# Turning tiles with 32x32 transposes on VectorE and copies inside SBUF, instead of transposes on TensorE

## Chip, core, metric

One core of a Trainium2 chip. The metric is the device time of one execution in microseconds (us). Every kernel here ran several times. Ratios to the kernel before are the mean time of the one kernel's fast runs over that of the other's fast runs of the same rounds, so they are not quite the ratios of the medians that are quoted.

## The reference, cut to what matters

64 graphs of 256 nodes with 256 features pass through four layers of graph networks. Each starts with the same norm and adds its result to `x`:

```python
h = jnp.maximum(_layernorm(x, axis=-1), 0.0)
x = x + layer(h, adj, ...)
# layer 0: 8-head attention with a mask;  layer 1: one-head graph attention
# layer 2: three steps of message passing and a GRU cell, on the state h
#   m = h @ weight[i];  aggr = A^T m;  h = gru(aggr, h)
# layer 3: 4-head graph attention
```

All is float32. The kernel takes two graphs at a time, a "pair": 32 pairs of 4 tiles of 128 tokens each (T = 4, D = 256, P = 128, N2 = 512).

## The kernel before

The kernel's code hands its matmuls operands whose summed dimension lies on the partitions, and the products with weights sum over the features. So every normalised tile is turned, from tokens on the partitions to features on the partitions. In layer 2 the state is kept with features on the partitions, and is turned back into tokens after each step. Both turns are TensorE transposes into PSUM, evicted by VectorE or ScalarE.

```python
        for g in range(2):                      # in norm_relu_T; tokens=True in layer 2 only
            def scaled(g=g):                    # (x - mean) * rstd: ScalarE if tokens, else VectorE
                ...
        hT = w4()
        for k in range(2):
            ps = bank()
            def turn(k=k, ps=ps):
                for t in range(T):
                    nc.tensor.transpose(ps()[:, t * P : (t + 1) * P], tok(xn())[:, t, k * P : (k + 1) * P], ident)
            add((PE, 4 * TURN, turn), reads=[xn], writes=[ps], claims=[hT])
            ...                                 # evicted, with the ReLU, to hT[:, k, :]
# in layer2, after each of the three steps:
            for g in range(2):
                ps = bank()
                def tokens(g=g, ps=ps, hT=hT):  # 4 transposes of the state
                    ...
                add((PE, 4 * TURN, tokens), reads=[hT], writes=[ps], claims=[h] if h else [])
                ...                             # evicted to h, or added to x after the last step
```

The order of all instructions is made while the program is built. Each task is given to `add` with an engine, the time that it is taken to occupy that engine, and a latency until its result can be read. The ordering then takes, again and again, the task that can begin first, over several pairs at once, and emits the tasks in that order.

```python
    def add(self, forms, reads=(), writes=(), latency=0.0, claims=()):
        ...
            free[engine] = begin + us                                   # in order()
            t.begin, t.end, t.engine = begin, begin + us + t.latency, engine
...
    SLOTS = {   # tag: (tiles, shape, type, tiles kept back for the oldest pair)
        "adj": (2, [P, T * N], I32, 1),
        "w4": (20, [P, T * D], FP, 6),
        "w8": (4, [P, 8, N], FP, 1),
        "mask": (4, [P, T * N], BF, 1),
        "ps": (8, [P, 512], FP, 2),
        ...
```

## Time and profile before

| | before |
|---|---|
| time, median of 3 | 4326.73 us (4326.27 to 4327.57) |
| TensorE busy, granted clock | 98%, 0.996 |
| VectorE, ScalarE, GpSimd busy | 68%, 53%, 14% |
| f32 transposes removed by the change | 1,792 |

In the lines shown, L414 is line 414 of that kernel's file, `w` stands for its 4 KB tiles, and SPq is SyncE's queue. An issue is the instruction that starts one copy. Its landing is counted from the start of the issue until the data are there. The granted clock is the share of full speed that TensorE's clock had.

The prediction below shows the lines. In TensorE's rows the end of one matmul overlaps the start of the next (in the run before, a 512-wide matmul of L761 has 0.59 us, and the next starts 0.43 us after it), so the measure used throughout is the distance between the starts of successive matmuls.

### The profile page before, as it was taken

The numbers are of one execution on the slowest core, as the hardware profiler recorded it, in microseconds if no ns is written. First come the engines' busy times: TensorE is split into PE (matmuls) and PEld (weight loads), VectorE is DVE, ScalarE is ACT, GpSimd is POOL, SyncE is SP. The second block draws the span as 40 slices with busy tenths as digits, with TensorE's granted clock in tenths as the row PEclk, the third lists the DMA queues.
The fourth block names the chain that finished last, engine by engine and source line by source line (L and its number), as shares of the span: only waits on it lengthen the run. The fifth ranks groups of instructions, "written<-read, shape, count | busy, mean of one in ns | idle before, by whom it ended". The sixth has DMA issues, their size and how long they took to land.

```text
span 4324.5 us, 56216 instructions
## 1 busy us (share of the span) xinstructions
PE 4244.1 (98%) x20720; PEld 2631.3 (61%) x20720; DVE 2930.0 (68%) x5426; ACT 2301.1 (53%) x6105; POOL 590.3 (14%) x582
## 2 busy tenths in 40 slices
PE   7999999999999999999999999999999999999997
PEld 5665566656656665666566566656655665666564
DVE  6775577667657755876676577558765765776554
ACT  4664465545545644655455456446554554564444
POOL 1111111111111111111111111111111111111111
PEclk9999999999999999999999999999999999999999
DMA  2000011000000000010000000000100100000000
GB/s 83 21 18 22 20 36 34 20 16 24 30 25 25 13 28 25 30 35 20 11 30 30 25 25 13 27 25 26 40 11 17 32 30 25 25 13 28 15 15 15
DMA packets 109986, 108.47 MB, mean 25 GB/s; under 512 B 7312, under 2 KB 109712, under 8 KB 109712
## 3 DMA queue, kind: packets, MB, share of 16 engines
q1 hardware_dynamic: 109712, 104.89, 7.6%
q8 instruction: 163, 2.67, 0.3%
q14 instruction: 111, 0.91, 0.1%
HBM read 88.09 MB, written 16.78 MB: 24 GB/s over the span
## 4 chain that ended last, share of the span: by engine, by line
PE 77%; DVE 8%; issue 8%; ACT 5%; POOL 1%; SPq 0%; DMA 0%; POOLq 0%; ACTq 0%; DVEq 0%
PE ps L761 36%; PE ps L775 7%; PE ps L518 5%; PE ps L480 5%; PE ps L573 4%; PE ps L717 3%; PE ps L654 3%; PE ps L540 2%; PE ps L457 2%; PE ps L614 2%; PE ps L840 2%; PE ps L858 2%; ACT w L886 2%; ACT w L494 2%; DVE w L823 1%
## 5 line engine op out<-in xcount | busy, mean ns | idle before, releaser
L761 PE MATMUL ps<-w,whhT 128*128 128x512 f32 x2304 | 1080.3, 595 | 0.7 <-DVE w L402 0.4
L761 PE MATMUL ps<-w,giT 128*128 128x512 f32 x2304 | 1063.6, 593 | 0.0
L494 ACT ACTIVATE w<-w,mx 128x256 f32<-128x256 f32 x1664 | 825.7, 503 | 186.3 <-DVE mx L561 128.9
L401 ACT COPY w<-ps 128x512 f32<-128x512 f32 x983 | 553.0, 587 | 657.3 <-PE ps L775 290.8
L761 PEld LDWEIGHTS ps<-w,giT 128*128 128x128 f32 x2304 | 433.6, 190 | 523.9 <-issue 513.3
L761 PEld LDWEIGHTS ps<-w,whhT 128*128 128x128 f32 x2304 | 415.3, 190 | 406.6 <-issue 383.9
L811 POOL TENSOR_TENSOR w<-w,w 128x512 f32<-128x512 f32 x192 | 251.2, 1317 | 1689.6 <-ACT w L806 1331.8
L402 DVE COPY w<-ps 128x512 f32<-128x512 f32 x553 | 366.4, 684 | 153.7 <-PE ps L573 58.0
L786 ACT ACTIVATE w<-ps,brz 128x512 f32<-128x512 f32 x192 | 131.8, 687 | 463.2 <-PE ps L761 460.3
L791 DVE TENSOR_SCALAR w<-w 128x512 f32<-128x512 f32 x192 | 81.6, 425 | 407.8 <-ACT w L786 407.7
L554 DVE SCALAR_TENSOR_TENSOR w<-ps,mask 128x512 f32<-128x512 f32 x512 | 333.3, 680 | 33.9 <-PE ps L540 33.9
L775 PE MATMUL ps<-w,w 128*128 128x256 f32 x1536 | 355.7, 379 | 0.0
L775 PEld LDWEIGHTS ps<-w,w 128*128 128x128 f32 x1536 | 286.2, 190 | 60.7 <-issue 22.9
L494 ACT ACTIVATION_READ_ACCUMULATOR w<-w,mx 128x1 f32 x1664 | 322.9, 194 | 0.0
L823 DVE SCALAR_TENSOR_TENSOR w<-w,w 128x512 f32<-128x512 f32 x192 | 152.5, 794 | 246.3 <-ACT w L818 240.7
L561 DVE TENSOR_REDUCE mx<-w 128x4 f32<-128x1024 f32 x256 | 309.2, 1208 | 2.0
L573 PE MATMUL ps<-ident,w 128*128 128x128 f32 x2048 | 269.4, 273 | 0.6
L573 PEld LDWEIGHTS ps<-ident,w 128*128 128x128 f32 x2048 | 235.1, 140 | 57.1 <-issue 25.6
L818 ACT ACTIVATE w<-ps,brz 128x512 f32<-128x512 f32 x192 | 130.8, 681 | 235.0 <-PE ps L761 234.9
L424 POOL TENSOR_SCALAR rs<-mv 128x4 f32<-128x4 f32 x128 | 33.6, 262 | 1354.8 <-DVE mv L417 1293.5
L886 ACT ACTIVATE w<-w,f 128x256 f32<-128x256 f32 x512 | 217.1, 503 | 1.4
L445 DVE TENSOR_SCALAR w<-x,mv,rs 128x256 f32<-128x256 f32 x384 | 185.3, 541 | 16.5 <-POOL rs L425 15.8
(113 smaller groups left out, 5633.0 us busy)
## 6 DMA issues: line engine op xcount, KB each, us to landing
adj<-in_adj_dram SPq DMA_DIRECT2D x128, 512.0 KB, 4.1
x<-in_x_dram SPq DMA_DIRECT2D x64, 256.0 KB, 2.8
out_dram<-x SPq DMA_DIRECT2D x64, 256.0 KB, 2.2
gg_sb<-in_L_gnn_weight_dram SPq DMA_DIRECT2D x3, 256.0 KB, 3.7
wih_sb<-in_L_gnn_w_ih_dram SPq DMA_DIRECT2D x1, 768.0 KB, 6.9
whh_sb<-in_L_gnn_w_hh_dram SPq DMA_DIRECT2D x1, 768.0 KB, 8.6
wq_sb<-in_L_gnn_Wq_dram SPq DMA_DIRECT2D x1, 256.0 KB, 2.8
wk_sb<-in_L_gnn_Wk_dram SPq DMA_DIRECT2D x1, 256.0 KB, 3.0
```

Source lines behind the costliest of these rows:

```text
L401: (A, act(n), lambda: nc.scalar.copy(dst(), src())),
L402: (V, dve(n), lambda: nc.vector.tensor_copy(dst(), src())),
L480: mm(ps()[:, c * D : (c + 1) * D], chunk(src, k, 2 * g + c), rhs[:, k, :], start=k == 0, stop=k == 1)
L494: nc.scalar.activation(tok(e(), N)[:, i, :], tok(e(), N)[:, i, :], AF.Exp, bias=mx()[:, m : m + 1], accum_out=zs()[:, z : z + 1],)
L518: mm(ps(), w[:, k, o * P : (o + 1) * P], tok(hT(), N2)[:, k, :], start=k == 0, stop=k == 1)
L554: (V, dve(N2), lambda s=s, j=j, b=b, t=t: nc.vector.scalar_tensor_tensor(tok(s(), N)[:, 2 * j : 2 * j + 2, :], tok(b(), N), SCALE, tok(mb( ...
L561: (V, dve(4 * N), lambda s=s, mx=mx, h4=h4: nc.vector.tensor_reduce(mx()[:, h4], tok(s(), N), AX.X, ALU.max, negate=True)),
L573: nc.tensor.transpose(tok(ps(), P)[:, 2 * i + c, :], tok(s(), N)[:, 2 * k + i, c * P : (c + 1) * P], ident,)
L761: mm(ps(), w[:, k, c0 : c0 + P], at_o(src, k), start=n == 0, stop=n == 2 * len(terms) - 1)
L775: mm(ps()[:, g * N : (g + 1) * N], tok(h())[:, t, o * P : (o + 1) * P], tok(am(), N)[:, t, :], start=c == 0, stop=c == 1,)
L811: (G, pool(N2), lambda o=o, u=u, hT=hT, hn=hn: nc.gpsimd.tensor_sub(at_o(u, o), at_o(hT, o), at_o(hn, o))),
L886: (A, act(N, 1), lambda t=t, g=g, h=h, e=e: nc.scalar.activation(tok(e(), N)[:, h, :], tok(sd[h // 2](), N2)[:, h % 2, g * N : (g + 1) * N ...
```

## The change

The intent is to take 1,792 transposes off TensorE, the engine that sets the end. The changed code uses VectorE's transpose for every 32x32 block where it lies; 16 copies inside SBUF, one for each pair of 32-partition groups, then put the blocks in their places.

```diff
-        "adj": (2, [P, T * N], I32, 1),
-        "w4": (20, [P, T * D], FP, 6),
-        "w8": (4, [P, 8, N], FP, 1),
+        "adj": (3, [P, T * N], I32, 1),
+        "w4": (26, [P, T * D], FP, 6),
...
-        "mask": (4, [P, T * N], BF, 1),
+        "mask": (6, [P, T * N], BF, 1),
...
+    def turn(src, blocks, dst, piece):
+        for i in range(2):
+            add(
+                (V, dve(N2), lambda i=i: nc.vector.transpose(piece(blocks, i), piece(src, i))),
+                reads=[(src, i)], writes=[(blocks, i)],
+            )
+        def shuffle():
+            for a in range(4):
+                for b in range(4):
+                    nc.sync.dma_start(
+                        dst()[32 * b : 32 * b + 32].rearrange("p (m c j) -> p m c j", c=4, j=32)[:, :, a, :],
+                        blocks()[32 * a : 32 * a + 32].rearrange("p (m c j) -> p m c j", c=4, j=32)[:, :, b, :],
+                    )
+        add((SP, 7.8, shuffle), reads=[blocks], writes=[dst], latency=3.5)
...
     # norm_relu_T: TensorE's transposes and evictions go; the norm is always scaled on ScalarE, with the ReLU
+        turn(xn, w4() if tokens else xn, hT, lambda b, i: b()[:, i * N2 : (i + 1) * N2])
...
     # turned tiles lie token chunk first; chunk() and at_o() address them so
+    def at_o(b, o):
+        return b().rearrange("p (t k j) -> p t k j", k=2, j=P)[:, :, o, :]
...
     # layer2, after each step:
+            h = w4()
+            turn(u, w4(), h, at_o)
+            if l == NL - 1:
+                add((V, dve(T * D), lambda h=h: nc.vector.tensor_add(xt(), h(), xt())), reads=[h], writes=[xt])
...
     # the 8 KB tiles of layers 0 and 3 become 4 KB tiles of the same pool
-            pT = [buf("w8") for half in range(2)]
+            pT = [w4() for i in range(4)]
```

In `add((SP, 7.8, shuffle), ..., latency=3.5)`, the ordering takes a turn to hold SyncE's queue for 7.8 us and to be readable 3.5 us later.

More of the change, by code (lines that the diff above doesn't have):

```diff
@@ L427, in norm_relu_T @@
         add((G, 1.4, rstd), reads=[mv], writes=[(rs, 0)])
-        xn = w4()
-        if tokens:
-            add(
-                (V, 0.17, lambda: nc.vector.scalar_tensor_tensor(
-                    rs()[:, 1, :], mv()[:, :, 0], -1.0, rs()[:, 0, :], ALU.mult, ALU.mult)),
-                reads=[mv, (rs, 0)], writes=[(rs, 1)],
-            )
+        add(
+            (V, 0.07, lambda: nc.vector.scalar_tensor_tensor(
+                rs()[:, 1, :], mv()[:, :, 0], -1.0, rs()[:, 0, :], ALU.mult, ALU.mult)),
+            reads=[mv, (rs, 0)], writes=[(rs, 1)],
+        )
+        xn, hT = w4(), w4()
         for g in range(2):
@@ L438, in scaled @@
                 for t in (2 * g, 2 * g + 1):
-                    if tokens:
-                        nc.scalar.activation(
-                            tok(xn())[:, t, :], tok(xt())[:, t, :], AF.Relu,
-                            bias=rs()[:, 1, t : t + 1], scale=rs()[:, 0, t : t + 1],
-                        )
-                    else:
-                        nc.vector.tensor_scalar(
-                            tok(xn())[:, t, :], tok(xt())[:, t, :], mv()[:, t, 0:1], rs()[:, 0, t : t + 1],
-                            ALU.subtract, ALU.mult,
-                        )
-            add((A, 0.95, scaled) if tokens else (V, 0.75, scaled), reads=[(xt, g), mv, rs], writes=[(xn, g)])
-        hT = w4()
-        for k in range(2):
-            ps = bank()
-            def turn(k=k, ps=ps):
-                for t in range(T):
-                    nc.tensor.transpose(ps()[:, t * P : (t + 1) * P], tok(xn())[:, t, k * P : (k + 1) * P], ident)
-            add((PE, 4 * TURN, turn), reads=[xn], writes=[ps], claims=[hT])
-            dst = lambda k=k: tok(hT(), N2)[:, k, :]
-            if tokens:
-                add(evict(N2, dst, ps), reads=[ps], writes=[(hT, k)])
-            else:
-                add(
-                    [
-                        (A, act(N2), lambda dst=dst, ps=ps: nc.scalar.activation(dst(), ps(), AF.Relu)),
-                        (V, dve(N2), lambda dst=dst, ps=ps: nc.vector.tensor_scalar_max(dst(), ps(), 0.0)),
-                    ],
-                    reads=[ps], writes=[(hT, k)],
-                )
+                    nc.scalar.activation(
+                        tok(xn())[:, t, :], tok(xt())[:, t, :], AF.Relu,
+                        bias=rs()[:, 1, t : t + 1], scale=rs()[:, 0, t : t + 1],
+                    )
+            add((A, 0.95, scaled), reads=[(xt, g), mv, rs], writes=[(xn, g)])
+        turn(xn, w4() if tokens else xn, hT, lambda b, i: b()[:, i * N2 : (i + 1) * N2])
         return (at, hT, xn) if tokens else (at, hT)
     def chunk(hT, k, t):
-        return tok(hT(), N2)[:, k, t * P : (t + 1) * P]
+        return hT().rearrange("p (t k j) -> p t k j", k=2, j=P)[:, t, k, :]
+    def at_o(b, o):
+        return b().rearrange("p (t k j) -> p t k j", k=2, j=P)[:, :, o, :]
     def graph_mm(ps, src, rhs, g):
@@ L517, in product @@
                     for k in range(2):
-                        mm(ps(), w[:, k, o * P : (o + 1) * P], tok(hT(), N2)[:, k, :], start=k == 0, stop=k == 1)
+                        mm(ps(), w[:, k, o * P : (o + 1) * P], at_o(hT, k), start=k == 0, stop=k == 1)
                 add((PE, 1.72, product), reads=[hT], writes=[ps], claims=[dst])
@@ L576, in turn @@
                                     )
-                        add((PE, 4 * TURN, turn), reads=[s], writes=[ps], claims=[pT[half]])
+                        add((PE, 4 * TURN, turn), reads=[s], writes=[ps], claims=[pT[2 * half + k]])
                         add(
@@ L581, in layer0 @@
                                 N2,
-                                lambda half=half, k=k, ti=ti, pT=pT: pT[half]()[:, 4 * k : 4 * k + 4, ti * P : (ti + 1) * P],
+                                lambda dst=pT[2 * half + k], ti=ti: tok(dst(), N)[:, :, ti * P : (ti + 1) * P],
                                 lambda ps=ps: tok(ps(), P),
                             ),
-                            reads=[ps], writes=[(pT[half], (ti, k))],
+                            reads=[ps], writes=[(pT[2 * half + k], ti)],
                         )
@@ L616, in context @@
                                 tok(v())[:, 2 * g + c, h * D0 : (h + 1) * D0],
-                                pT[hh // 2]()[:, 4 * (hh % 2) + 2 * cc + c, :],
+                                tok(pT[hh](), N)[:, 2 * cc + c, :],
                                 start=c == 0,
@@ L624, in layer0 @@
                 (V, dve(N2), lambda g=g, psc=psc, rzT=rzT: nc.vector.tensor_tensor(
-                    tok(cT(), N2)[:, :, g * N : (g + 1) * N], tok(psc(), N), tok(rzT(), N), ALU.mult)),
+                    cT()[:, g * N2 : (g + 1) * N2].rearrange("p (t k j) -> p k t j", k=2, j=P),
+                    psc().rearrange("p (k t j) -> p k t j", k=2, j=P),
+                    rzT().rearrange("p (k t j) -> p k t j", k=2, j=P), ALU.mult)),
                 reads=[psc, rzT], writes=[(cT, g)],
@@ L751, in layer2 @@
             r, hn, u = w4(), w4(), w4()
-            at_o = lambda b, o: tok(b(), N2)[:, o, :]
             def gate(us, terms, c0, o, claims=()):
@@ L760, in do @@
                         for k in range(2):
-                            mm(ps(), w[:, k, c0 : c0 + P], at_o(src, k), start=n == 0, stop=n == 2 * len(terms) - 1)
+                            mm(tok(ps(), P), w[:, k, c0 : c0 + P], at_o(src, k), start=n == 0, stop=n == 2 * len(terms) - 1)
                             n += 1
@@ L780, in layer2 @@
                 add((PE, 1.73, messages), reads=[h, am], writes=[ps], claims=[aT])
-                add(evict(N2, lambda o=o, aT=aT: at_o(aT, o), ps), reads=[ps], writes=[(aT, o)])
+                add(evict(N2, lambda o=o, aT=aT: at_o(aT, o), lambda ps=ps: tok(ps(), P)), reads=[ps], writes=[(aT, o)])
             both = ((whhT, hT), (giT[:, l], aT))
@@ L786, in layer2 @@
                     (A, act(N2, 1), lambda o=o, ps=ps, r=r: nc.scalar.activation(
-                        at_o(r, o), ps(), AF.Tanh, bias=brz[:, o : o + 1], scale=0.5)),
+                        at_o(r, o), tok(ps(), P), AF.Tanh, bias=brz[:, o : o + 1], scale=0.5)),
                     reads=[ps], writes=[(r, o)],
@@ L795, in layer2 @@
                     (V, dve(N2) + 0.07, lambda o=o, ps=pshn[o], r=r, hn=hn: nc.vector.scalar_tensor_tensor(
-                        at_o(hn, o), ps(), bhh_sb[:, 4 + o : 5 + o], at_o(r, o), ALU.add, ALU.mult)),
+                        at_o(hn, o), tok(ps(), P), bhh_sb[:, 4 + o : 5 + o], at_o(r, o), ALU.add, ALU.mult)),
                     reads=[pshn[o], (r, o)], writes=[(hn, o)],
@@ L801, in layer2 @@
                 add(
-                    (V, dve(N2), lambda o=o, ps=ps, hn=hn: nc.vector.tensor_add(at_o(hn, o), ps(), at_o(hn, o))),
+                    (V, dve(N2), lambda o=o, ps=ps, hn=hn: nc.vector.tensor_add(at_o(hn, o), tok(ps(), P), at_o(hn, o))),
                     reads=[ps], writes=[(hn, o)],
@@ L818, in layer2 @@
                     (A, act(N2, 1), lambda o=o, ps=ps, r=r: nc.scalar.activation(
-                        at_o(r, o), ps(), AF.Tanh, bias=brz[:, 2 + o : 3 + o], scale=0.5)),
+                        at_o(r, o), tok(ps(), P), AF.Tanh, bias=brz[:, 2 + o : 3 + o], scale=0.5)),
                     reads=[ps], writes=[(r, o)],
@@ L832, in layer2 @@
             hT = u
-            h = w4() if l < NL - 1 else None
-            for g in range(2):
-                ps = bank()
-                def tokens(g=g, ps=ps, hT=hT):
-                    for c in range(2):
-                        for k in range(2):
-                            nc.tensor.transpose(ps()[:, c * D + k * P : c * D + (k + 1) * P], chunk(hT, k, 2 * g + c), ident)
-                add((PE, 4 * TURN, tokens), reads=[hT], writes=[ps], claims=[h] if h else [])
-                if h is None:
-                    add_to_x(xt, g, ps)
-                else:
-                    add(evict(N2, lambda g=g, h=h: h()[:, g * N2 : (g + 1) * N2], ps), reads=[ps], writes=[(h, g)])
+            h = w4()
+            turn(u, w4(), h, at_o)
+            if l == NL - 1:
+                add((V, dve(T * D), lambda h=h: nc.vector.tensor_add(xt(), h(), xt())), reads=[h], writes=[xt])
     def layer3(xt, p):
@@ L879, in layer3 @@
             zs, rz = buf("zs"), buf("rz")
-            eT = buf("w8")
+            eT = [w4() for k in range(2)]
             for ti in range(2):
@@ L911, in turn @@
                                 )
-                    add((PE, 4 * TURN, turn), reads=[e], writes=[ps], claims=[eT])
+                    add((PE, 4 * TURN, turn), reads=[e], writes=[ps], claims=[eT[k]])
                     add(
@@ L916, in layer3 @@
                             N2,
-                            lambda k=k, ti=ti, eT=eT: eT()[:, 4 * k : 4 * k + 4, ti * P : (ti + 1) * P],
+                            lambda dst=eT[k], ti=ti: tok(dst(), N)[:, :, ti * P : (ti + 1) * P],
                             lambda ps=ps: tok(ps(), P),
                         ),
-                        reads=[ps], writes=[(eT, (ti, k))],
+                        reads=[ps], writes=[(eT[k], ti)],
                     )
@@ L932, in product @@
                                 f()[:, 2 * g + c, h * C3 : (h + 1) * C3],
-                                eT()[:, 2 * h + c, :],
+                                tok(eT[k](), N)[:, 2 * j + c, :],
                                 start=c == 0,
@@ L936, in product @@
                             )
-            add((PE, 1.86, product), reads=[eT, (f, 2 * g), (f, 2 * g + 1)], writes=[pso], claims=[oT])
+            add((PE, 1.86, product), reads=[*eT, (f, 2 * g), (f, 2 * g + 1)], writes=[pso], claims=[oT])
             add(evict(N2, oT, pso), reads=[pso], writes=[oT])
```

## The prediction

> **What bounds the kernel now.** I read the page from the top: busy shares (part 1), then the slices (part 2), then the groups.
>
> ```profile
> PE 4244.1 (98%) x20720; PEld 2631.3 (61%) x20720; DVE 2930.0 (68%) x5426; ACT 2301.1 (53%) x6105; POOL 590.3 (14%) x582
> ...
> PE   7999999999999999999999999999999999999997
> ```
>
> TensorE has work in every slice but the first and the last; VectorE is next with 68%. A busy matmul row includes a modelled end that overlaps the next one, so 98% alone proves little. The distances between starts do. The timeline, 2006 to 2009 us (start, length, engine, line, what):
>
> ```profile
> 2006.62 0.19 PEld L761 LDWEIGHTS ps<-w,giT 128*128 128x128 f32 x1 [0.24 <-issue]
> 2007.04 0.19 PEld L761 LDWEIGHTS ps<-w,giT 128*128 128x128 f32 x1 [0.24 <-issue]
> 2007.47 0.14 PEld L457 LDWEIGHTS ps<-ident,w 128*128 128x128 f32 x1 [0.24 <-issue]
> ...
> 2007.90 1.04 PE L457 MATMUL ps<-ident,w 128*128 128x128 f32 x8
> ...
> 2008.67 0.90 PEld L573 LDWEIGHTS ps<-ident,w 128*128 128x128 f32 x8
> 2008.77 1.04 PE L573 MATMUL ps<-ident,w 128*128 128x128 f32 x8
> ```
>
> A 512-wide f32 matmul instruction follows its predecessor after 0.43 us. Eight transposes of L457 take from 2007.90 to 2008.77, 0.109 us each, and the next group starts at once. So a transpose costs 0.109 us of TensorE, not the 0.273 us of its row. Taking such start distances for every group over the whole trace (4,608 gate matmuls x 0.429 = 1977, 1,536 messages x 0.216 = 332, all 6,015 f32 transposes x 0.109 = 656, the rest 1,210) I get about 4175 us of the 4324.5 us span. The 150 us left are some 40 before the first pair, some 25 at the end, and small waits. The kernel is bound by the sum of TensorE's work.
>
> The two groups that the change removes, in the groups by shape (busy us, mean ns, then idle before):
>
> ```profile
> L457 PE MATMUL ps<-ident,w 128*128 128x128 f32 x1024 | 141.0, 277 | 13.0 <-issue 7.2 <-DVE w L445 4.7 <-ACT w L440 0.9
> L840 PE MATMUL ps<-ident,w 128*128 128x128 f32 x768 | 105.6, 277 | 13.8 <-DVE w L828 11.3 <-ACT w L606 2.5
> ```
>
> And the DMA side (page part 3 and the issues; KB each, us to landing):
>
> ```profile
> q1 hardware_dynamic: 109712, 104.89, 7.6%
> ...
> out_dram<-x SPq DMA_DIRECT2D x64, 256.0 KB, 2.2
> ...
> b_sb<-in_L_gnn_b_dram SPq DMA_DIRECT2D x1, 1.0 KB, 2.2
> ```
>
> The DMA engines are nearly empty. An issue on the queue of SyncE takes 0.37 to 0.39 us in the view of that line (medians 0.380 to 0.394), and one follows another after 0.50 us at the kernel's start. `b_sb` is 256 pieces of 4 bytes and lands after 2.2 us, no later than 256 pieces of 1 KB (`out_dram`): the number of pieces is not dear.
>
> [...] No VectorE transpose is in the trace before. [...] The trace's single packets take 46 ns (1,024 bytes) and 9 ns (4 bytes) in the median[...]; no 128-byte piece and no SBUF-to-SBUF copy is there to test it.
>
> **The change part by part.**
>
> *TensorE.* 32 pairs x 4 layers x 8 = 1,024 transposes (L457) and 32 x 3 x 8 = 768 (L840) go: 1,792 x 0.109 = 195 us, all on the engine that sets the end. Matmuls keep their number and widths; their moving operand is now four runs of 128, for which I charge nothing. With them go 14 fillings of PSUM banks a pair, and the 27 us of idle time the two rows show ahead of them, of which I count 15.
>
> *VectorE.* Added: 7 turns x 32 pairs x 2 = 448 block transposes x 0.68 = 305; 96 small L431 operations x 0.153 = 15; 32 additions of 1,024 elements x about 1.2 (as L892) = 38. Removed: L445 185 (to ScalarE), L467 50, half of L634 42, and of the 192 evictions of turned tiles by the general copy some 36% (553 of 1,536 go to VectorE) x 0.68 = 47. Net +34: 2964 us, 71% of a span of 4175. Not a bound.
>
> *ScalarE.* Added 384 x 0.592 (L440) = 227; removed L466 66 and about 123 evictions x 0.587 = 72. Net +89: 2390 us, 57%.
>
> *SyncE's queue.* 224 turns x 16 = 3,584 copies. At 0.42 to 0.50 us each a turn takes 7 to 8 us to issue, 1,500 to 1,800 us together, some 40% of the span. It is one queue in program order, so turns of two pairs that coincide wait for each other.
>
> *DMA engines.* A turn moves 128 x 4 KB in 128-byte pieces: 4,096, so 256 on each engine. Between 9 and 46 ns I interpolate 14 ns for 128 bytes (an estimate): 3.5 us a turn, less than its issue. In all 917,504 x 14 / 16 = 0.8 ms, about a fifth of the span.
>
> *Latency of a turn.* Now: in the timeline the last scaled rows of L445 end at 2003.99 and the second eviction ends at 2009.63, 5.6 us, because TensorE works in order. Afterwards: transposes 1.3 (side by side with nothing), issue 7 to 8, landing 2.5, so 11 to 12 us. 6 us more per turn, 7 turns: some 40 us more in a pair's chain, which has about 510 us (four `x` tiles, a pair leaves every 127 us or so). In mid-kernel other pairs, and the matmuls on the untransposed state, cover nearly all of it; I charge 30 us for what is not covered, and for TensorE's waits on up to 16 copies a turn. At the end nothing covers it: the last pair's states and layer 3's norm come one after another, and TensorE already sits idle there (2.19, 2.19, 4.66 us ahead of L840 and L457 in the timeline). Three or four turns of 8 to 10 us, partly hidden by the state's own matmuls: +25.
>
> *Buffers.* 20 four-KB tiles and 4 of eight KB (28 equivalents) become 26 in one pool; the mask and adjacency tiles grow. Any shortage is inside the 30.
>
> Sum: 4327 - 195 - 15 + 30 + 25 = 4172; I put 4170.
>
> **Rivals.**
>
> 1. *Latency starves TensorE.* For: each turn holds two or three tiles for 11 us instead of two for 5.6, a pair in layer 0 already needs about 13 of them, and the pool has two fewer in bytes. Against: layer 2 gives TensorE about 72 us of work a pair (144 x 0.429 + 48 x 0.216), in steps long enough to hide another pair's turn, and one pool can lend where two could not. It would give 4230 to 4300.
> 2. *Copies are slower than taken.* If a 128-byte piece cost what a 1,024-byte one does (46 ns), a turn would need 256 x 46 = 11.8 us of every engine, more than its issue; 224 x 11.8 = 2.6 ms would still fit under the span, but with queueing a turn would take 16 us and more, and program order on the queue would hold up loads. That gives 4250 to 4400. Against: the 4-byte pieces.
> 3. *All latency is hidden and PSUM gets roomier.* The freed banks end some of the small waits among the 150 us: 4327 - 195 - 40, about 4090.
> 4. *VectorE becomes the bound.* At 71% it can do so only in stages (softmax of layers 0 and 3); if block transposes took twice 0.68 us it would stand at 78%. Some tens of us at most.
>
> **Range and chances.** The 195 us are firm to within 10. The added waits could lie between -20 and +150. So 4100 to 4290, leaning to the low side. Faster by over 2% means below about 4240, lost only if rival 1 or 2 holds fully: 0.80. Within 2%: 0.15. Slower: 0.05.
>
> **What would show it.** TensorE's instructions fall by 1,792 and its start distances sum to about 3980 us; its busy share stays at 95% or more in the inner slices; VectorE stands near 2960 us and a block transpose near 0.68 us; the copies are issued every 0.42 to 0.5 us and the last lands some 2.5 us after its issue; DMA share rises to 20 or 30%. Wrong it would be if the inner slices of PE fall to 8 or less with matmuls waiting for DMA, if packets of 128 bytes take over 30 ns, or if SyncE's queue is occupied for most of the span.

## The result, and the profile after

The changed kernel took 4495.65 us (median of 4, 4493.67 to 4496.37), 1.0389 of the time before (95% interval 1.0371 to 1.0407). It is slower by 3.9%; the forecast was 4170 us, and the measured time lies above the range.

The page of the changed kernel: busy times, slices, DMA queue, the issues of the copies.

```profile
PE 4160.3 (93%) x18928; PEld 2484.1 (55%) x18928; DVE 2912.9 (65%) x5367; ACT 2371.1 (53%) x6292; POOL 589.1 (13%) x582
...
PE   6999989999999989899999999999999999999985
...
q1 hardware_dynamic: 1084560, 222.56, 23.7%
...
PE 50%; SPq 23%; DVE 12%; ACT 8%; issue 4%; DMA 3%; POOL 0%; DVEq 0%; ACTq 0%; POOLq 0%
...
L414 DVE STREAM_TRANSPOSE w<-w 128x512 f32<-128x512 f32 x448 | 307.8, 699 | 66.8 <-ACT w L459 62.9
...
w<-w SPq DMA_DIRECT2D x3584, 32.0 KB, 1.9
```

TensorE has 1,792 instructions fewer, as intended, but is busy for 93% only. VectorE and ScalarE are no busier than forecast, the DMA engines are under a quarter used. What is new is in the fourth line, the chain that ended last: 23% of the span runs through SyncE's queue. The same line before the change has 0% there:

```profile
PE 77%; DVE 8%; issue 8%; ACT 5%; POOL 1%; SPq 0%; DMA 0%; POOLq 0%; ACTq 0%; DVEq 0%
```

The instructions of the copies' line, by their own duration (ns, min/median/max):

```profile
L421 SPq DMA_DIRECT2D w<-w x3584: 585/609/2046, 53.0 to 4458.5; - x200
L421 SPq EVENT_SEMAPHORE  x316: 17/28/33626, 48.2 to 4440.2; - x158
...
DMA to landing us min/median/max: 1.9/1.9/5.3
```

One issue holds the queue for 0.609 us and the next starts 0.653 us after it. From the first issue of a turn to the end of its last, the median over 224 turns is 10.40 us (mean 10.72, 2,401 us together), where the ordering had 7.8. From the first issue to the landing of the last, the median is 11.7 us, where the ordering had 7.8 + 3.5 = 11.3. So a turn that finds the queue free is hardly longer than planned; it is the time for which it holds the queue that exceeds the plan by a third.

A turn's first issue came 4.1 us after the end of its block transposes in the mean (paired in order of time), and over 2 us late for 101 of the 224. Of these 923 us together, 848 us lie under the issues of another turn: the turns queue behind each other.

How that reaches TensorE shows in the chain of waits, 2040 to 2070 us (start, length, what):

```profile
2040.61 0.64 DVE w L414
2041.39 0.59 SPq L421
...
2051.18 0.61 SPq L421
2051.79 0.05 issue
2051.90 0.58 SPq L421
...
2061.02 0.61 SPq L421
2061.68 1.92 DMA w<-w
2063.60 0.09 issue
2063.69 6.72 PE ps L516 x8
```

The first turn's sixteenth issue starts at 2051.18; the second turn's sixteen issues start from 2051.90 to 2061.68. The last of them lands at 2063.60, and only then can TensorE begin with the queries of layer 0. The timeline of TensorE there:

```profile
2057.30 1.88 PE L760 MATMUL ps<-w,whhT 128*128 128x512 f32 x4
2059.02 1.88 PE L760 MATMUL ps<-w,giT 128*128 128x512 f32 x4
2063.69 6.72 PE L516 MATMUL ps<-w,wq_sb 128*128 128x512 f32 x8 [2.79 <-DMA w<-w]
2070.25 3.60 PE L516 MATMUL ps<-w,wk_sb 128*128 128x512 f32 x8
```

TensorE stood for 2.79 us. The eight matmuls behind it then took 6.72 us, while the same eight, for the keys, took 3.60 us. The clock record has half clock from 2063.00 to 2069.83 us: it set in 0.69 us before the stand ended and lasted nearly to the end of the eight. The record of this run has 51 half-clock stretches, 311 us together, against 5 of 37 us before. All but the last, which the end of the span cuts, last a multiple of 3.413 us. Of the 51, 50 began during a stand of over 1 us (29) or within 1.5 us of its end (21), counted from the end of one matmul's row to the start of the next. The mean granted clock is 0.966 against 0.996.

The waits of TensorE for turned tiles (total us, times, longest):

```profile
PE ps L516 <- DMA w<-w: 58.7, 12, 22.7
...
PE ps L847 <- DMA w<-w: 35.4, 2, 34.7
...
PE ps L774 <- DMA w<-w: 28.4, 10, 10.6
PE ps L760 <- DMA w<-w: 23.8, 7, 5.6
PE ps L654 <- DMA w<-w: 20.3, 10, 4.8
```

These are the first readers of a turned tile in layers 0, 3, 2, 2 and 1; none of these waits existed before. The 22.7 us lie at the start of the kernel and the 34.7 us at its end.

For a sum I take the distances between the starts of successive matmuls. A group's own distance is its median ("work"; for the two packed groups of 32-row and 32-column matmuls, the mean of those under 200 ns). What exceeds it inside a half-clock stretch, up to one own distance, is "slow"; the rest is "stands". The stands contain a few hundred us of small distances in every kernel, so read differences.

| us | work | stands | slow | sum | span |
|---|---|---|---|---|---|
| before | 4051 | 392 | 8 | 4451 | 4324.5 |
| after | 3854 | 665 | 101 | 4620 | 4494.6 |
| difference | -197 | +273 | +93 | +169 | +170.1 |

(The sums exceed the spans, because packed matmuls with a start a few ns apart are counted with their mean. The differences close.) The work went as forecast. Stands and half clock took back 366 us. Gaps of over 1 us alone rose from 20 of 43 us to 87 of 302 us; 252 us of those lie ahead of the five first readers. What is left of the stands, the small distances, hardly differs (349 us before, 363 after, 340 in the run eight below), so the waits of TensorE on sixteen copies a turn instead of eight cost no more than some 25 us.

### The profile page after: what moved, and what is told of

It is laid out like the page before. It is cut to its first block, busy times and chain, and to the rows that moved or that the text cites. A ratio compares the mean times of both kernels' runs of the same rounds, so it can differ in the third digit from the quotient of the medians.

```text
span 4494.6 us, 58450 instructions
## 1 busy us (share of the span) xinstructions
PE 4160.3 (93%) x18928; PEld 2484.1 (55%) x18928; DVE 2912.9 (65%) x5367; ACT 2371.1 (53%) x6292; POOL 589.1 (13%) x582
## 3 DMA queue, kind: packets, MB, share of 16 engines
q1 hardware_dynamic: 1084560, 222.56, 23.7%
## 4 chain that ended last, share of the span: by engine, by line
PE 50%; SPq 23%; DVE 12%; ACT 8%; issue 4%; DMA 3%; POOL 0%; DVEq 0%; ACTq 0%; POOLq 0%
PE ps L760 23%; SPq L421 22%; PE ps L774 4%; PE ps L516 4%; ACT w L492 3%; DMA w<-w 3%; PE ps L478 2%; PE ps L571 2%; PE ps L654 2%; PE ps L847 2%; ACT w L875 2%; PE ps L919 2%; PE ps L898 2%; DVE w L552 2%; DVE w L414 1%
## 5 line engine op out<-in xcount | busy, mean ns | idle before, releaser
L760 PE MATMUL ps<-w,whhT 128*128 128x512 f32 x2304 | 1105.5, 607 | 52.7 <-DMA w<-w 23.8
L760 PE MATMUL ps<-w,giT 128*128 128x512 f32 x2304 | 1084.0, 599 | 1.6 <-DVE w L401 1.6
L400 ACT COPY w<-ps 128x512 f32<-128x512 f32 x903 | 503.6, 584 | 742.6 <-PE ps L774 205.4
L774 PE MATMUL ps<-w,w 128*128 128x256 f32 x1536 | 372.5, 394 | 44.9 <-DMA w<-w 28.4
L401 DVE COPY w<-ps 128x512 f32<-128x512 f32 x441 | 292.7, 681 | 153.7 <-PE ps L571 52.7
L459 ACT ACTIVATE w<-x,rs 128x256 f32<-128x256 f32 x512 | 266.4, 590 | 217.0 <-DVE rs L450 202.6
L774 PEld LDWEIGHTS ps<-w,w 128*128 128x128 f32 x1536 | 296.0, 197 | 114.0 <-issue 47.0
L414 DVE STREAM_TRANSPOSE w<-w 128x512 f32<-128x512 f32 x448 | 307.8, 699 | 66.8 <-ACT w L459 62.9
L805 ACT ACTIVATE w<-w,bih_sb 128x512 f32<-128x512 f32 x192 | 136.3, 718 | 238.5 <-DVE w L801 238.3
L946 POOL TENSOR_TENSOR x<-w,x 128x512 f32<-128x512 f32 x64 | 82.9, 1295 | 1194.0 <-DVE w L941 951.9
```

Source lines behind the costliest of these rows:

```text
L400: (A, act(n), lambda: nc.scalar.copy(dst(), src())),
L401: (V, dve(n), lambda: nc.vector.tensor_copy(dst(), src())),
L414: (V, dve(N2), lambda i=i: nc.vector.transpose(piece(blocks, i), piece(src, i))),
L459: nc.scalar.activation(tok(xn())[:, t, :], tok(xt())[:, t, :], AF.Relu, bias=rs()[:, 1, t : t + 1], scale=rs()[:, 0, t : t + 1],)
L760: mm(tok(ps(), P), w[:, k, c0 : c0 + P], at_o(src, k), start=n == 0, stop=n == 2 * len(terms) - 1)
L774: mm(ps()[:, g * N : (g + 1) * N], tok(h())[:, t, o * P : (o + 1) * P], tok(am(), N)[:, t, :], start=c == 0, stop=c == 1,)
```

## The experiments

Two theories stood at first. **A**: the turns by DMA are too long, either for the order that was built with 7.8 and 3.5 us (A1), or in any order (A2). **B**: the rest of the change costs the time: one pool, the layout, the norm on ScalarE. A third, **C**, says that any detour over VectorE and a DMA starves TensorE. All kernels give correct results unless "wrong" is said.

| run | time, us | ratio | a turn on SyncE's queue, then landing, us | stands + slow |
|---|---|---|---|---|
| after | 4495.65 | 1.0389 | 10.4, 1.9 | 665 + 101 |
| pe_turns | 4341.08 | 1.0032 | none | 393 + 22 |
| replan | 4355.82 | 1.0065 | 10.4, 1.9 | 569 + 56 |
| eight (wrong) | 4188.08 | 0.9681 | 5.3, 2.1 | 436 + 25 |
| dram_own | 4194.73 | 0.9693 | 5.9, 3.1 | 446 + 22 |
| one_copy (wrong) | 4248.87 | 0.9818 | 0.5, 3.2 | 474 + 45 |
| contig (wrong) | 4333.04 | 1.0013 | 10.1, 1.8 | 552 + 45 |
| sh_spare | 4290.07 | 0.9916 | 10.4, 1.9 | 514 + 45 |
| split2 | 4245.70 | 0.9815 | 8.1, 1.9 | 494 + 22 |
| pe_spare | 4284.83 | 0.9904 | none | 350 + 9 |
| dram2 | 4166.76 | 0.9632 | 5.6, 3.1 | 426 + 12 |

### pe_turns: all of the change but the turns

```diff
-        turn(xn, w4() if tokens else xn, hT, ...)      # and for the states
+        for i in range(2):                              # 4 TensorE transposes into a bank, then an eviction
+            add((PE, 4 * TURN, blocks_on_pe), reads=[src], writes=[ps], claims=[dst])
+            add(evict(N2, lambda i=i: dst()[:, i * N2 : (i + 1) * N2], ps), reads=[ps], writes=[dst])
```

> All of the change (one pool of 26 tiles, token chunk first, norm scaled on ScalarE) but the turns, which are again TensorE's transposes with evictions. Theory A (the turns by DMA are the loss): 4300 to 4350 us, as before, clock 0.99. Rival B (pool, layout or the norm on ScalarE lose the time): 4420 us or more.

Measured 4341.08 us, 1.0032 of before. Theory B falls: pool, layout and the norm on ScalarE together cost 0.3%. The rest of the loss sits in the turns.

### replan: the same instructions, ordered with the measured figures

```diff
-        add((SP, 7.8, shuffle), reads=[blocks], writes=[dst], latency=3.5)
+        add((SP, 10.5, shuffle), reads=[blocks], writes=[dst], latency=2.0)
```

> The changed kernel, whose list of tasks is ordered with 10.5 us of SyncE's queue and 2.0 us of landing for a turn (measured: 10.4 us of issue in the median, 1.9 us) in place of 7.8 and 3.5. Instructions and their number stay. Theory A1 (the order was built on a turn that is too short, so TensorE runs into turns that are not done): most of the loss goes, the time falls to 4290 to 4340 us, gaps of TensorE over 1 us from 301 us to under 150, half-clock time from 311 us to under 120. Theory A2 (the length of a turn costs this, in any order): at least 4420 us.

Measured 4355.82 us, 1.0065 of before. The same copies, as slow as before (0.609 us an issue, 10.4 us a turn), in another order are 140 us faster. That rejects A2 in its strong form. It misses A1's window by 16 us, and the gaps over 1 us (208 us) and the half-clock time (222 us) stay above what A1 asked: the right order gets back most of the loss, not the gain. The turns queue as before (first issue 4.3 us late in the mean, 99 over 2 us late), so the 140 us do not come from less queueing. What differs is that this order reckons with it.

### eight: the order of the changed kernel, shorter turns (wrong)

```diff
-            for a in range(4):
-                for b in range(4):
-                    nc.sync.dma_start(dst()[32 * b : 32 * b + 32]..., blocks()[32 * a : 32 * a + 32]...)
+            for a in range(2):
+                for b in range(2):
+                    for c in range(2):                  # 64 rows a copy; planned with 7.8 and 3.5 as before
+                        nc.sync.dma_start(dst()[64 * b : 64 * b + 64]..., blocks()[64 * a : 64 * a + 64]...)
```

> Wrong on purpose: the changed kernel in its own order (planned with 7.8 us of queue and 3.5 us of landing), but a turn is 8 copies of 64 rows in place of 16 of 32 rows; every copy still touches all eight column blocks, so a reader still waits for all of them. At 0.6 us each a turn occupies the queue for about 5 us, less than planned. If the loss of the changed kernel is that the real turn (10.4 us of queue) is longer than the one that the order was built on, the time falls to 4180 to 4270 us, with the gaps of TensorE over 1 us below 150 us in total. If the order itself is bad whatever a turn takes, it stays above 4400 us.

Measured 4188.08 us, 0.9681 of before, with gaps over 1 us of 96 us in all. The line of the copies:

```profile
L417 SPq DMA_DIRECT2D w<-w x1792: 590/633/1968, 50.9 to 4153.2; - x200
...
DMA to landing us min/median/max: 2.0/2.1/4.5
```

An issue of 64 rows took no less than one of 32 (0.633 us against 0.609), but there are half as many. The bytes and pieces moved are the same: 917,504 pieces of 128 bytes. The order is the same in fact: the traces of this run, of dram_own and of contig have, on TensorE, VectorE, ScalarE and GpSimd, the same sequence of instructions as the changed kernel (18,928, 5,367, 6,292 and 582, compared by line of code, operation, tile names and shape). So neither bytes nor pieces, but the number of issues, made the turn long (10.4 us of queue with sixteen, 5.3 with eight); and with turns inside the planned length the very order that lost 3.9% wins 3.2%.

### dram_own: the order of the changed kernel, a shorter way, correct results

The turn goes by way of HBM: the pattern `v[b]` on the HBM side takes rows of all partitions, so five issues do what sixteen did (224 out and 896 back in the trace, for 3,584).

```diff
-        def shuffle(): ...                              # 16 copies
+        def by_hbm():
+            nc.sync.dma_start(room(), blocks())         # 128 rows of 4 KB to HBM
+            v = room().rearrange("(a q) (m b j) -> b q m a j", a=4, b=4, j=32)
+            for b in range(4):                          # 128-byte pieces back
+                nc.sync.dma_start(dst()[32 * b : 32 * b + 32].rearrange("p (m a j) -> p m a j", a=4, j=32), v[b])
+        add((SP, 7.8, by_hbm), reads=[blocks], writes=[room, dst], latency=3.5)
```

> The changed kernel in its own order (a turn planned with 7.8 us of queue and 3.5 us of landing, tiles kept back as there), correct results; only the way of a turn differs: one copy out to HBM, a wait for its landing, four copies back. From the run before with this way: 0.7 + 2.6 + 2.7 us on the queue, then some 3 us of landing, so about 9 us in all against 11.3 planned and 12.3 of the sixteen copies. If the order held only a turn of the planned length, as the run with eight copies says: 4180 to 4230 us. If that run was fast because its data were wrong or its copies covered 64 rows: 4350 us or more.

Measured 4194.73 us, 0.9693 of before. This confirms the run before without its wrong data. The expectation's 12.3 us for the sixteen copies counts the last issue twice, since a landing is counted from the start of its issue: it is 11.7 us, against 8.6 here and 11.3 planned. The larger difference is in the queue, which a turn holds for 5.9 us here and for 10.4 there, with 7.8 planned; a turn's first issue is 1.3 us late in the mean here and 4.1 there. With turns that fit the plan the time comes within 25 us of the forecast (4170); with turns that hold the queue longer it is 300 us more.

### one_copy: a single plain copy in place of sixteen (wrong)

```diff
-        def shuffle(): ...                              # 16 copies; (SP, 7.8, ...), latency=3.5
+        def shuffle():
+            nc.sync.dma_start(dst(), blocks())
+        add((SP, 0.7, shuffle), reads=[blocks], writes=[dst], latency=3.0)
```

> Wrong on purpose: the 16 copies of a turn are one plain copy of 128 rows of 4 KB, planned with 0.7 us of queue and 3.0 us of landing; the block transposes stay. Theory A (queue time of 16 issues): a turn takes 5 us and the gain that was predicted appears, 4150 to 4230 us. Rival C (any detour over VectorE and a DMA, with its tiles held, starves TensorE): over 4300 us.

Measured 4248.87 us, 0.9818 of before: between the two expectations. Theory C is rejected as the main cause, since the detour stays and the time is below before. But the shortest turn of all is not the fastest kernel. Its order is another one, and there TensorE has 75 us of gaps over 1 us ahead of the transposes of layer 3, whose releaser is ScalarE's exponentials, and only 35 us ahead of first readers of turned tiles. Two orders can differ by some tens of us for reasons that have nothing to do with turns by DMA (pe_turns and pe_spare, which have none, are 56 us apart); that is why the two runs in the changed kernel's own order weigh most.

### contig: sixteen copies of 1 KB rows (wrong, inconclusive)

```diff
-                        dst()[32 * b : 32 * b + 32].rearrange(...)[:, :, a, :],
-                        blocks()[32 * a : 32 * a + 32].rearrange(...)[:, :, b, :],
+                        dst()[32 * b : 32 * b + 32, a * D : (a + 1) * D],
+                        blocks()[32 * a : 32 * a + 32, b * D : (b + 1) * D],
```

> Wrong on purpose: the same 16 copies of 32 KB per turn in the same plan as the changed kernel, but each moves 32 rows of 1 KB without gaps instead of 256 pieces of 128 bytes. If the 0.61 us of an issue (0.38 us for a load) come from the pattern's dimensions or pieces, an issue falls to about 0.4 us, a turn to 7 us, and with the plan's 7.8 us true again the time is 4150 to 4230 us. If every copy from SBUF to SBUF costs 0.6 us, issue and time stay: 4450 to 4520 us.

An issue took 0.588 us (minimum 0.507), against 0.609 with the gaps, so the gaps in the pattern are not what made an issue dear. The time, 4333.04 us from two runs, fits neither branch. The edit changed a second thing: each copy now touches a quarter of the columns, so waits become finer. On SyncE's queue the wait instructions rose from 316 to 1,058, and 44 turns began before their second block transpose had ended, which no turn of the changed kernel does. By its layout a reader, likewise, need not wait for all 16 copies; whether it gained by that was not measured. The order is that of the changed kernel. How the 160 us divide between this and the slightly shorter turn (10.05 us) was not separated.

### sh_spare: the sixteen copies, measured figures, other tiles kept back

```diff
-        "w4": (26, [P, T * D], FP, 6),
+        "w4": (26, [P, T * D], FP, 3),
-        add((SP, 7.8, shuffle), reads=[blocks], writes=[dst], latency=3.5)
+        add((SP, 10.5, shuffle), reads=[blocks], writes=[dst], latency=2.0)
```

> The changed kernel's 16 copies, ordered with the measured 10.5 and 2.0 us as in the run before, and with 3 in place of 6 of the 26 tiles kept back for the oldest pair. The kernel's own plan then ends at 4211 us in place of 4284 us; planned and measured times differed by 72 us in the run with the measured figures. If what is left of the loss is a matter of order and of tiles: 4260 to 4300 us, so faster than before by 1%. If the 10.4 us of queue per turn are a floor of their own: 4340 us or more.

Measured 4290.07 us, 0.9916 of before. With an order that knows their length, the sixteen copies are a small gain. The control pe_spare below reaches the same with TensorE's turns, so no gain of the copies themselves is shown in this form (pe_spare also keeps back one bank less, so the two choices are not quite alike).

### split2: four of the sixteen issued by ScalarE

```diff
-        add((SP, 7.8, shuffle), reads=[blocks], writes=[dst], latency=3.5)
+        add((SP, 10.5 * 0.75, lambda: shuffle(nc.sync, (0, 1, 2))), reads=[blocks], writes=[(dst, "s")], latency=2.0)
+        add((A, 10.5 * 0.25, lambda: shuffle(nc.scalar, (3,))), reads=[blocks], writes=[(dst, "a")], latency=2.0)
```

(5 of the tiles and 1 of the banks are kept back.)

> The same 16 copies, 12 issued by SyncE (7.9 us planned) and 4 by ScalarE (2.6 us); 5 tiles kept back, plan 4143 us. If the time of the issue on one queue is what costs: a turn takes 8 to 9 us and the time is 4180 to 4240 us; ScalarE gets 540 us more of issuing. If ScalarE's tasks wait behind its issues [...]: 4300 us or more.

Measured 4245.70 us, 0.9815 of before, 6 us outside the first window. The part on SyncE's queue fell to 8.1 us a turn; the other expectation, 4300 us or more because ScalarE's tasks would wait behind its issues, did not come. But this run also keeps back other tiles and banks than sh_spare, so how much of the 44 us between them comes from the queue was not separated.

### pe_spare: the control for the choice of what is kept back

```diff
     # pe_turns, and:
-        "w4": (26, [P, T * D], FP, 6),
+        "w4": (26, [P, T * D], FP, 7),
-        "ps": (8, [P, 512], FP, 2),
+        "ps": (8, [P, 512], FP, 1),
```

> The control for the fast version: turns on TensorE as in the run with all of the change but the turns, with the tiles kept back chosen as well as they can be there (7 of the 26, 1 of the banks); its plan ends at 4254 us instead of 4294 us. If the fast version owes its gain to the choice of what is kept back: under 4200 us. If it owes it to TensorE's 195 us: 4280 to 4310 us.

Measured 4284.83 us, 0.9904 of before. Choosing what is kept back is worth 1.3% by itself (4341 to 4285).

### dram2: by way of HBM, in an order of its own

```diff
+        add((SP, 0.65, lambda: nc.sync.dma_start(room(), blocks())), reads=[blocks], writes=[room], latency=2.5)
+        add((SP, 2.6, back), reads=[room], writes=[dst], latency=2.5)     # the four copies of dram_own
-        "w4": (26, [P, T * D], FP, 6),
+        "w4": (26, [P, T * D], FP, 5),
-        "ps": (8, [P, 512], FP, 2),
+        "ps": (8, [P, 512], FP, 1),
```

> The turn by way of HBM: one copy of 128 rows of 4 KB out, then four copies that read 128-byte pieces back, 5 issues in place of 16; planned with 0.65 us and 2.5 us of landing out, 2.6 us and 2.5 us back; plan 4088 us. If the number of issues is the price of a turn: SyncE's queue is taken for about 3.5 us a turn, and the time is 4120 to 4190 us, faster than before by 3 to 5%. If pieces of 128 bytes from HBM are slow (over 30 ns a piece), the landing goes past 6 us and the time past 4250 us.

Measured 4166.76 us (4164.02 to 4171.45), 0.9632 of before, correct: faster than both kernels. Its page and its issues:

```profile
PE 4042.4 (97%) x18928; PEld 2437.8 (59%) x18928; DVE 2911.4 (70%) x5364; ACT 2377.5 (57%) x6295; POOL 590.9 (14%) x582
...
q1 hardware_dynamic: 1073808, 339.84, 33.2%
...
room<-w SPq DMA_DIRECT2D x224, 512.0 KB, 2.6
w<-room SPq DMA_DIRECT2D x896, 128.0 KB, 3.1
```

It moves half as many bytes again as the sixteen copies did (339.84 against 222.56 MB), and is faster, because a turn is 5 issues: 0.34 us out (median), then four of 0.68 us. By these medians the issues add up to 224 x (0.34 + 4 x 0.68) = 685 us, against 3,584 x 0.609 = 2,183 us. TensorE is back at 97%, clock 0.991. Against pe_spare, where what is kept back was also chosen (7 tiles there, 5 here, 1 bank in both), the turns by HBM are worth 118 us (4284.83 - 4166.76).

## Why the prediction was wrong

*TensorE's 195 us:* right. The work between starts fell by 197 us.

*VectorE and ScalarE:* right. VectorE 2913 us busy (forecast 2964), ScalarE 2371 (2390), a block transpose 0.70 us (0.68, an estimate from the 128x512 operations of L402 and L735, 684 and 676 ns in the mean of the trace before). VectorE did not become the bound, so rival 4 fell.

*DMA engines:* right. A 128-byte piece took 12 ns in the median of the packet records (forecast 14, estimated between the 9 ns of 4 bytes and the 46 ns of 1,024 bytes), the queue's share is 23.7% (20 to 30), the last copy lands 1.9 us after its issue (2.5). Rival 2, slow pieces, named the wrong cost. The 256 pieces on each engine were an estimate, an even split over the page's 16 engines, which no trace showed. One reading behind it was not sound, though: `b_sb` and `out_dram` have 256 pieces each, so that they land after the same 2.2 us says that the size of a piece mattered little there, and nothing of their number.

*SyncE's queue:* here it failed. The step "At 0.42 to 0.50 us each a turn takes 7 to 8 us to issue" was taken from loads of 128 rows (0.38 to 0.39 us an instruction). A 32-row copy inside SBUF holds the queue for 0.609 us and the pitch is 0.653 us, so a turn takes 10.4 us and the 224 turns 2,401 us, 53% of the span instead of 40%. The profile before held the warning. The prediction used the landing of `b_sb`, but not its issue, nor those of the eight small copies ahead of it:

```profile
13.01 6.78 SPq L334 DMA_DIRECT2D blk<-in_L_gnn_a_dram  x8
19.83 0.59 SPq L350 DMA_DIRECT2D b_sb<-in_L_gnn_b_dram  x1
```

The median of those eight, one element on each of 64 rows, is 0.595 us, and where nothing came between them they started every 0.64 us. Sixteen at that pace would have been estimated at 15 x 0.64 + 0.60 = 10.2 us. The prediction noted that "turns of two pairs that coincide wait for each other" and gave it no time; the wait is 4.1 us in the mean.

*Latency of a turn:* the step "I charge 30 us for what is not covered", with 25 for the end, holds the term of the sum that was mis-sized: stands and half clock rose by 366 us. The 25 us for the end were right: over the last 130 us of the span stands and half clock rose by 32 us. It is the 30 us for the middle of the kernel that failed: between the first and the last 130 us they rose by some 320 us. And they failed because of the queue: in eight and dram_own, whose turns hold it for no longer than planned, the middle rose by 24 and 28 us. Two things were missed. First, the order is fixed with 7.8 us for a turn, the same optimistic figure that I had arrived at from the loads; I never asked what a fixed order does when one of its figures is short. Other pairs' work covers a turn only where the order has put such work, and TensorE took nothing else meanwhile (the 18,928 instructions of TensorE have one sequence in the four runs). Replan (-140 us with the same copies), eight and dram_own (-300 us with the same order) show this from both sides. Second, the stands of TensorE cost more than themselves: the half-clock stretches that came with them added 93 us.

*Rival 1*, latency that starves TensorE, is what happened, but its size (4230 to 4300 us) was not right, nor was its reason, too few tiles, the main one: eight, dram_own and replan have the same 26 tiles. (Tiles have a share: sh_spare differs from replan only in keeping back 3 of them instead of 6, and is 66 us faster.)

*The signs:* of the three that were to show the prediction wrong, two came: four of the 38 inner slices of TensorE fell to 8, with matmuls waiting for copies, and SyncE's queue was occupied for most of the span (53%). Packets of 128 bytes did not take over 30 ns (12 ns in the median).

*Buffers:* pe_turns shows that the pool and the layout cost no more than 0.3%, as assumed. That the choice of tiles kept back is worth 1.3% was not foreseen.

What stays open: why an issue costs 0.61 us for 32 rows inside SBUF and 0.47 us for 128 rows; how much of contig's gain is finer waits; and how what replan does not get back divides between the longer turns and its order.

## What to carry to other kernels

Where an order is fixed ahead with assumed durations, measure the duration of a new kind of task on the chip before trusting the order; if the real one is longer, the order itself can be the loss (140 of 169 us here), and re-ordering with the measured figure is the first repair. A transfer cut into many small copies was priced here by its issues on one queue: count issues, not bytes, take their time from the smallest copies in the profile (0.595 us before, 0.609 us after), and look for a route that needs fewer, even one that moves more bytes (here 339.84 MB in place of 222.56). When TensorE stands, look at the clock record too: here half clock cost 93 us on top of the stands' 273.

## What the runs measured of issues, pieces and transposes

- In the changed kernel the sixteen issues of a turn took 10.4 us, and the last landed 1.9 us after its issue.
- The issue times, in the median, are 0.34 us (128 rows, SBUF to HBM, dram2), 0.38 to 0.39 us (loads and stores of 128 rows, before), 0.47 us (128 rows inside SBUF, one_copy), 0.61 us (32 rows inside SBUF, after), 0.63 us (64 rows inside SBUF, eight) and 0.68 us (HBM to 32 rows, dram2).
- A 128-byte piece took 12 ns inside SBUF, and a 1,024-byte piece of the loads and stores in the same trace 46 ns (10.7 against 22 bytes per ns). For the pieces from HBM in dram2 I estimate 18 ns at most: 33.2% of 16 engines over 4,165.9 us, less 102,400 pieces of 1,024 bytes at their mean of 52 ns in the changed kernel, over 917,504 pieces.
- A 128x512 f32 block transpose on VectorE took 0.70 us, about as long as a copy of that size (0.68 us).
- The rows of an f32 transpose on TensorE show 273 to 277 ns, but in a stream one starts every 109 ns, and that is what removing one saved (197 us for 1,792).
